# An FNO block and a dilation on one core: the first layer's product with x and its spectral rows as one pass of 32x32 matmuls

## The chip, the cores and the metric

The kernel runs on 1 core of one Trainium2 chip. The metric is the device time of one execution in microseconds (us). Several runs of each kernel are timed, and the median is given. One more execution is profiled, and its trace is what the profile is read from.

## The reference, cut to what matters

The input x has 8 images of 8 channels and 256 x 256 pixels. There are two stages, each with a group norm in front and a residual behind it.

```
x = x + L0(gn(x))        # lift 2 -> 10 channels per group, 4 Fourier layers, two pointwise layers
x = x + dilate(gn(x))    # maximum of a 3x3 window, border -2

L0(x):
  h = W0 @ [x, gridx, gridy] + b0                    # 4 groups, each 2 channels and 2 grids -> 10
  for i in 0..3:
    h1 = irfft2(R_i * rfft2(h), 12 + 12 rows and 12 columns of modes kept)
    h  = h1 + (W_i @ h + b_i);  h = swish(h) if i < 3
  h = swish(W_fc1 @ h + b)                           # 10 -> 128 per group
  return W_fc2 @ h + b                               # 128 -> 2 per group
```

The lift is linear, so the kernel never stores its result: layer 0 takes x itself, with the product of the two weights (`wc`), and the grids and biases enter as two extra rows of the spectral part.

## The kernel before, in words

The state of one image is the tile `h`: 128 partitions, 11 chunks (`NCH`), 4 quarters and 512 pixels, that is two rows of the image. A strip of 32 partitions holds 3 blocks of 10 channels. All data are float32, and each matmul of the program shows as two LDWEIGHTS and two MATMUL instructions in the profile.

Each image passes through four layers (`layers`, L505). Before a layer, `spectrum_h` (or, for layer 0, `spectrum_x`, L218) and `mix` (L345) compute the modes of the layer's output and write them to `fz`. There column 24 of the 32 columns holds a constant and column 25 a ramp. `rows_of` (L390) expands them to one set of 32 coefficients for each image row, in `zt`; it uses all 32 columns of `fz` against the table `rowg`. The columns 26 to 31 are zero.

`layer` (L416) then goes over the 11 chunks. `burst(c)` (L442) makes the layer's output for a chunk in two PSUM tiles. In layer 0 it first multiplies x by `wcn` (L449: 16 matmuls with 6 rows, 32 columns of weights and 512 pixels), where `wcn` is `wc` times the norm's factor (L476). Then it adds the spectral part (L455: 8 matmuls of the coefficients `zt`, 32 rows by 128, with the waves `binv`, 256 columns, 32 rows of which 26 are not zero). In the layers 1 to 3 the first product is with the state itself (L452). ACT applies the activation and writes `h` back in place (L461; L463 in layer 3). `turn(c-1)` (L424) transposes the chunk before, and `transform(c-2)` (L437) takes its row transform for the next layer.

After layer 3 a chunk goes to HBM (`stored`, L465). The two pointwise layers, `head` (L568), read it back in 256 KB tiles `hs` (L580) and work in 128 steps an image, two matmul groups (L588, L610) and two activations (L590) a step; a DVE addition (L615) follows every second step. These steps are woven into the layers of the next image: a generator yields numbers, and the main loop (L698 to L731) runs so many steps of `head` in between (`CHUNK` = 2, 1, 1 per chunk in the first three layers, `LAST` = 2 in layer 3). The dilation (`dilate`, L639) follows in the layers after that. It works in pieces of two rows: one transfer in (`yin`, L646), eight or so DVE operations, one transfer out (L674), both on POOL's queue. The start of the next image's layer 0, `spectrum_x` and its `mix`, runs within layer 3 of the image before (`start`, L498).

PE, DVE and ACT take their instructions in the order in which the program writes them (`manual_schedule`). The framework orders the DMA queues of SP and POOL itself, by its own estimate of when each transfer can begin. `read_x` (L467) loads the rows of x into `h`, 4 transfers of 6 rows by 8 KB for each chunk, all on SP's queue. They are written at the head of layer 0, and a chunk of `h` is free for them once the image before has stored it. SP's queue also has the stores, the `hs` loads, the spectral weights `t` (L342), x for the norm (L73) and x for the residual (L603).

One pool of four PSUM tiles (`ps_z`, two banks each) serves everything: a burst, a turn and a head step's L588 take two each, all else takes one.

Of the kernel before, what the change touches and what calls it, by code (L numbers as in the profile page):

```python
# [20 lines left out]
G = 4  # L21
# [17 lines left out]
STEPS = 128  # L39
CHUNK = (2, 1, 1)  # L40
LAST = (2,)
SIDE = 4.2


@with_exitstack
def fno_dilate_kernel(ctx: ExitStack, tc: tile.TileContext, a: dict, out: bass.AP):
# [42 lines left out]
    fc0c = load("fc0c", (128, 3))  # L89
    wbd = load("wbd", (128, WID, G))  # L90
    wt = load("wt", (128, 4, G, 32))
    eh0 = load("eh0", (128, 3, 2, 32), nc.sync)
    xe = load("xe", (128, 6, G, 5), nc.sync)
    wext = const.tile([128, G, WID, 5], F32, tag="c_wext", name="c_wext")
# [10 lines left out]
    edge = load("edge", (128, 4))  # L105

    h = const.tile([128, NCH, NQ, PIX], F32, tag="h", name="h")
    yin = const.tile([128, DR + 2, HW + 2], F32, tag="yin", name="yin")
    nc.vector.memset(yin, -BIG)
    y_rows = [dram.tile([C * HW + 2, HW], F32, tag=f"y{i}", bufs=1, name=f"y_rows{i}") for i in range(2)]  # L110
# [7 lines left out]

    def softplus(t, n, name):
        e = const.tile([128, n], F32, tag=f"{name}_e", name=f"{name}_e")
# [5 lines left out]
        sp = const.tile([128, n], F32, tag=f"{name}_sp", name=f"{name}_sp")  # L128
# [3 lines left out]
        rs = const.tile([128, n], F32, tag=f"{name}_rs", name=f"{name}_rs")  # L132
# [6 lines left out]
    sp_p, rs_p = softplus(beta_p, 4, "bp")  # L139
    sp_a, rs_a = softplus(beta_a, 4 * G, "ba")  # L140
    io = const.tile([128, 4 * G], F32, tag="io", name="io")
    nc.vector.tensor_copy(io[:, 0:4], sp_a[:, 0:4])
    nc.vector.tensor_tensor(io[:, 4:12], sp_a[:, 4:12], rs_a[:, 0:8], ALU.mult)
# [3 lines left out]
        nc.vector.tensor_scalar(w2[:, g, :], w2[:, g, :], rs_a[:, 12 + g : 13 + g], None, ALU.mult)  # L147


    wc = const.tile([128, 32], F32, tag="wc", name="wc")  # L150
    p = ps_z("p_wc")
    for g in range(G):
        mm(p[32 * g : 32 * g + 6, 0, :32], fc0x[part(g), :], wt[part(g), 0, g, :], start=True, stop=True)
# [10 lines left out]
    cv = const.tile([3, WID, G], F32, tag="cv", name="cv")  # L164
# [180 lines left out]
    def mix(b, l, out_):  # L345

        s = [sb.tile([128, 3, G, 2, WID], F32, tag=f"S{i}", bufs=1, name=f"S{i}_{b}_{l}") for i in range(2)]
        bt, sw = out_["bt"], out_["sw"]
        for k in range(3):
            for k2 in range(2):  # L350
                pr = turned[:, 2, 1024 * k2 : 1024 * k2 + 800].rearrange("p (g m i) -> p g m i", g=G, i=WID)
                nc.vector.tensor_tensor(  # L352
                    pr, sw[k], bt[:, k2, k].unsqueeze(2).to_broadcast([128, G, 2 * WID, WID]), ALU.mult)
                yield 0.7
                nc.vector.tensor_reduce(  # L355
                    s[k2][:, k].rearrange("p g s o -> p (g s o)"),
                    pr.rearrange("p g m i -> p (g m) i"), AX.X, ALU.add,
                )
                if k == 0 and k2 == 1:
                    sw.append(load_sw(l, 2))  # L360
                yield 0.7
        f = sb.tile([128, 2, 3, G, WID], F32, tag="F", bufs=1, name=f"F_{b}_{l}")
        nc.vector.tensor_tensor(f[:, 0], s[0][:, :, :, 0, :], s[1][:, :, :, 1, :], ALU.subtract)
        nc.vector.tensor_tensor(f[:, 1], s[0][:, :, :, 1, :], s[1][:, :, :, 0, :], ALU.add)
        yield 0.5

        p = ps_a(f"p_f_{b}_{l}")
        for slot in range(2):
            for n, (table, part_of) in enumerate(((0, slot), (1 + slot, 1 - slot))):
                for q in range(4):  # L370
                    mm(p[part(q), 120 * slot : 120 * slot + 120], fold[part(q), table, :],
                       f[part(q), part_of].rearrange("p k g o -> p (k g o)"), start=n == 0, stop=n == 1)
        nc.vector.tensor_copy(fz[0:32, :, :, 24], cz[:, l])
        if l == 0:
            mr = out_["mr"]
            d = sb.tile([128, 1], F32, tag="d", name=f"dm_{b}")
            nc.vector.tensor_tensor(d, mr[:, 0:1], mr[:, 1:2], ALU.mult)
            mm(p[0:1, 240 : 240 + WID * G], d, wm.rearrange("p o g -> p (o g)"), start=True, stop=True)
            nc.vector.tensor_tensor(
                fz[0:1, :, :, 24], fz[0:1, :, :, 24],  # L380
                p[0:1, 240 : 240 + WID * G].rearrange("p (o g) -> p o g", o=WID), ALU.add)
        if l < 2:
            nc.vector.tensor_copy(fz[0:32, :, :, 25], cz[:, 4 if l == 0 else 3])
        for q in range(4):
            dst = fz[part(q), :, :, 6 * q : 6 * q + 6].rearrange("p o g k -> p k g o")
            src = p[part(q), :240].rearrange("p (k g o) -> p k g o", g=G, o=WID)
            copy(q, dst, src)
        yield 2.5
# [24 lines left out]
            yield 0.7  # L413


    def layer(b, l, out_, stored, side):  # L416
        group_in_f = l % 2 == 1

# [22 lines left out]

        def burst(c):  # L442
            pair = [ps_z(f"p_z_{b}_{l}_{c}_{i}") for i in range(2)]
            for f in range(NQ):
                for q in range(NQ):
                    o = pair[q // 2][part(f), q % 2, :]
                    if l == 0:
                        k = slice(32 * q, 32 * q + 6)
                        mm(o, wcn[k, :], h[k, c, f, :], start=True, stop=False)  # L449
                    else:  # L450
                        g = f if group_in_f else q
                        mm(o, wt[part(q), l, g, :], h[part(q), c, f, :], start=True, stop=False)  # L452
            for s in range(2):
                for q in range(NQ):
                    mm(pair[q // 2][:, q % 2, HW * s : HW * (s + 1)],  # L455
                       zt[part(q), 2 * c + s].rearrange("p f o -> p (f o)"), binv[part(q), :],
                       start=False, stop=s == 1)
            for i in range(2):
                dst = h[:, c, 2 * i : 2 * i + 2, :]
                if l < 3:  # L460
                    nc.scalar.activation(dst, pair[i], AF.Silu)  # L461
                else:
                    nc.scalar.activation(dst, pair[i], AF.Identity, bias=bias3)  # L463
            if l == 3:
                nc.sync.dma_start(stored[c], h[:, c].rearrange("p f w -> p (f w)"))  # L465

        def read_x(c):  # L467
            for g in range(G):
                nc.sync.dma_start(
                    h[32 * g : 32 * g + 6, c].rearrange("p f w -> p (f w)"), a["xp"][b, c, g])  # L470
# [48 lines left out]
    spare = h.rearrange("p c f w -> p (c f w)")  # L519
# [228 lines left out]
def _tables():  # L748
# [40 lines left out]
    binv[:, at + 3] = -c * np.sin(_angle(np.outer(ky, w)))  # L789
    binv[:, 2 * NM] = 1.0  # L790
    binv[:, 2 * NM + 1] = line


    planes = [np.broadcast_to(line[:, None], (HW, HW)), np.broadcast_to(line, (HW, HW)), np.ones((HW, HW))]
    xe = np.zeros((4, 32, 2, 3, G, 5))
    for j, v in enumerate(planes):
# [83 lines left out]
```

## Time and profile before

| what | us |
|---|---|
| median of 3 runs (4305.38 to 4307.73) | 4307.59 |
| the profiled execution | 4309.43 |
| its span, first to last instruction | 4307.7 |
| L590 ACT, 2048 activations, mean 1.025 | 1968.9 |
| L588 PE, matmuls of the first pointwise layer | 1191.6 |
| L610 PE, matmuls of the second | 986.7 |
| L424 PE, transposes | 525.8 |
| L455 PE, spectral part, all four layers, 5632 instructions | 408.6 |
| L452 PE, product with the state, layers 1 to 3 | 317.0 |
| L449 PE, product with x, layer 0, 2816 instructions | 115.0 |

HBM carries 344.65 MB in all, a mean of 80 GB/s; the mean granted clock of TensorE is 0.982 of full speed. Busy time is the union of a group's instructions. Matmuls overlap each other, so a group's mean length times its count says little, and its place in time is better read from the timeline, where equal instructions in a row are merged: start, length, engine, line, what it writes and reads, how many. The brackets give idle time of that engine before it and what ended it. In the table by stage a row has the stretch and its length, the busy time of PE, of its weight loads, of DVE, ACT and POOL, then the granted clock, the share of the DMA engines and GB/s.

### The profile page before, as it was taken

What the parts mean: (1) busy time and instruction counts of PE and PEld (TensorE: products, weight loads), DVE (VectorE), ACT (ScalarE), POOL (GpSimd) and SP (SyncE); (2) the same over time, 40 slices, a digit from 0 to 9 for tenths busy, and PEclk for the clock granted to TensorE, in tenths of its full rate; (3) what the DMA queues carried; (4) which work ended last, traced back from release to release, by engine and by line L of the source; (5) the groups of instructions that cost most, each with busy time, mean ns of one, the idle gap of its engine ahead of it and who ended that gap; (6) DMA issues with size and microseconds to landing.
All of it is one profiled execution on the core that took longest, in us unless ns stands there. A gap on an engine that the chain in (4) does not pass through costs nothing. (4 is left out here: it accounts for less than half of the span.)

```text
span 4307.7 us, 115455 instructions
## 1 busy us (share of the span) xinstructions
PE 4089.1 (95%) x52330; PEld 1925.6 (45%) x52330; DVE 2297.3 (53%) x3424; ACT 2772.9 (64%) x2886; POOL 117.0 (3%) x202
## 2 busy tenths in 40 slices
PE   5877999999999999999999999999999999999997
PEld 3544454444443444434444354444454444444222
DVE  4444544555655555655556555655655555654433
ACT  3435656766667666576666756667666766567887
POOL 1000000000000000000000000000000000000000
PEclk8988999999999999999999999999999999999999
DMA  2014101332114221242112511134111332114321
GB/s 78 13 40 151 53 28 43 135 103 62 55 53 161 87 62 52 75 171 58 52 59 81 182 42 53 50 104 159 55 45 53 136 120 62 48 57 147 109 60 46
DMA packets 113682, 344.65 MB, mean 80 GB/s; under 512 B 15611, under 2 KB 18107, under 8 KB 97768
## 3 DMA queue, kind: packets, MB, share of 16 engines
q1 hardware_dynamic: 95000, 276.18, 20.3%
q0 software_dynamic: 18192, 61.08, 4.3%
q8 instruction: 411, 6.73, 0.7%
q14 instruction: 79, 0.65, 0.1%
HBM read 213.21 MB, written 123.74 MB: 78 GB/s over the span
## 5 line engine op out<-in xcount | busy, mean ns | idle before, releaser
L590 ACT ACTIVATE act<-p_fc 128x1024 f32<-128x1024 f32 x2048 | 1968.9, 1025 | 1202.4 <-PE p_fc L588 1200.6
L588 PE MATMUL p_fc<-hs,c_w 32*128 32x512 f32 x8192 | 1191.6, 633 | 15.3 <-DVE turned L194 8.6
L610 PE MATMUL p_fc<-act,c_w 128*32 128x512 f32 x8192 | 986.7, 597 | 38.9 <-ACT act L590 25.6
L194 DVE COPY turned<-p_t 128x1024 f32<-128x1024 f32 x495 | 584.6, 1219 | 707.7 <-PE p_t L424 707.0
L588 PEld LDWEIGHTS p_fc<-hs,c_w 32*128 32x128 f32 x8192 | 383.6, 183 | 622.8 <-issue 240.9
L461 ACT ACTIVATE h<-p_z 128x1024 f32<-128x1024 f32 x528 | 512.9, 1023 | 117.4 <-PE p_z L455 116.7
L424 PE MATMUL p_t<-ident,h 128*128 128x128 f32 x4224 | 525.8, 278 | 0.0
L615 DVE TENSOR_TENSOR y<-p_fc,y 128x512 f32<-128x512 f32 x392 | 270.7, 690 | 474.9 <-PE p_fc L610 473.0
L610 PEld LDWEIGHTS p_fc<-act,c_w 128*32 128x32 f32 x8192 | 229.9, 109 | 647.4 <-issue 333.0
L424 PEld LDWEIGHTS p_t<-ident,h 128*128 128x128 f32 x4224 | 463.3, 142 | 98.5 <-ACT act L590 64.7
L455 PE MATMUL p_z<-c_binv,zt 32*128 32x256 f32 x5632 | 408.6, 404 | 1.0 <-ACT zt L192 1.0
L455 PEld LDWEIGHTS p_z<-c_binv,zt 32*128 32x128 f32 x5632 | 258.3, 185 | 304.4 <-issue 292.7
L452 PE MATMUL p_z<-h,c_wt 32*32 32x512 f32 x8448 | 317.0, 601 | 0.0
L437 PE MATMUL p_d<-turned,c_fw 128*32 128x240 f32 x4224 | 268.1, 371 | 4.1 <-ACT act L590 2.1
L194 DVE COPY zt<-p_g 128x264 f32<-128x264 f32 x300 | 159.0, 626 | 139.8 <-PE p_g L397 75.0
L463 ACT ACTIVATE h<-p_z,c_bias 128x1024 f32<-128x1024 f32 x176 | 186.6, 1111 | 26.4 <-PE p_z L455 25.9
L355 DVE TENSOR_REDUCE S<-turned 128x80 f32<-128x800 f32 x192 | 188.8, 983 | 5.0
L352 DVE TENSOR_TENSOR turned<-t,B 128x800 f32<-128x800 f32 x192 | 188.4, 981 | 0.5 <-DMA t<-in_spw 0.4
L452 PEld LDWEIGHTS p_z<-h,c_wt 32*32 32x32 f32 x8448 | 72.3, 103 | 190.1 <-ACT act L590 85.7
L437 PEld LDWEIGHTS p_d<-turned,c_fw 128*32 128x32 f32 x4224 | 109.6, 108 | 100.4 <-issue 39.1
L194 DVE COPY turned<-p_at 88x1024 f32<-88x1024 f32 x90 | 101.7, 1155 | 73.8 <-PE p_at L313 73.8
L438 DVE COPY zt<-p_d 128x240 f32<-128x240 f32 x264 | 105.5, 400 | 51.1 <-PE p_d L437 51.1
(170 smaller groups left out, 2023.8 us busy)
## 6 DMA issues: line engine op xcount, KB each, us to landing
stored<-h SPq DMA_DIRECT2D x88, 1024.0 KB
hs<-stored SPq DMA_DIRECT2D x352, 256.0 KB
t<-in_spw SPq DMA_DIRECT2D x96, 400.0 KB
yin<-y_rows POOLq DMA_DIRECT2D x56, 512.0 KB, 4.7
h<-in_xp SPq DMA_DIRECT2D x352, 48.0 KB
turned<-in_x SPq DMA_DIRECT2D x16, 1024.0 KB
y<-in_x SPq DMA_DIRECT2D x56, 256.0 KB
y_rows<-y POOLq DMA_DIRECT2D x56, 256.0 KB, 2.4
```

The lines of the kernel that those rows point to most:

```text
L194: nc.vector.tensor_copy(dst, src)
L352: nc.vector.tensor_tensor(pr, sw[k], bt[:, k2, k].unsqueeze(2).to_broadcast([128, G, 2 * WID, WID]), ALU.mult)
L355: nc.vector.tensor_reduce(s[k2][:, k].rearrange("p g s o -> p (g s o)"), pr.rearrange("p g m i -> p (g m) i"), AX.X, ALU.add,)
L424: nc.tensor.transpose(t[:, i // 4, 128 * (i % 4) : 128 * (i % 4 + 1)], h[:, c, i // 2, 256 * (i % 2) + 128 * v : 256 * (i % 2) + 128 * (v ...
L437: mm(p[part(g), :240], fw[:, v, :], m[:, :, :, : NBLK * WID], start=v == 0, stop=v == 1)
L452: mm(o, wt[part(q), l, g, :], h[part(q), c, f, :], start=True, stop=False)
L455: mm(pair[q // 2][:, q % 2, HW * s : HW * (s + 1)], zt[part(q), 2 * c + s].rearrange("p f o -> p (f o)"), binv[part(q), :], start=False, s ...
L461: nc.scalar.activation(dst, pair[i], AF.Silu)
L588: mm(pair[g // 2][:, g % 2, :], w1[part(g), blk, :], hs[k][part(g), :], start=True, stop=True)
L590: nc.scalar.activation(act[:, 2 * i : 2 * i + 2, :], pair[i], AF.Silu)
L610: mm(acc[part(g), :], w2[:, g, 15 - rb - i : 47 - rb - i], act[:, g, :], start=i == 0, stop=i == 1)
L615: nc.vector.tensor_tensor(y, sums, y, ALU.add)
```

## The change

In layer 0 the two products become one. The 32 rows of a strip of `h` now hold 26 rows of waves (the first 26 rows of `binv`, repeated for the 8 image rows of a chunk) and 6 rows of x. The weight of x becomes six more columns of `fz`, 26 to 31, which `rows_of` spreads to `zt` through three new rows of `rowg`. A burst is 2 x 16 matmuls of 32 x 32 weights from `zt` with 256 columns of `h`, each its own accumulation group; L455 no longer runs in layer 0.

The waves come from a new table in HBM by 4 transfers of 26 x 8 KB for each chunk, on POOL's queue. The x rows stay on SP's queue, 4 transfers a chunk, now to the partitions 26 to 31 of each strip. Both are written in the program for the first four chunks ahead of `rows_of`, and for the chunk c+4 ahead of burst c.

The new columns of `fz` are made once an image in the `mix` of layer 0: a DVE scaling (`wsel`), 4 small matmuls into two PSUM tiles and two DVE copies. `wcn` goes. At the start of the program there are three more DVE operations (`ws`, `wk`) and one more table; a few small start-up tiles move into a part of `h`.

```diff
+    xrow = load("xrow", (128, 38))
...
-    wc = const.tile([128, 32], F32, tag="wc", name="wc")
+    wc = spare[:, 22400:22432]
...
+    ws = spare[:, 22472:22482]
+    nc.vector.tensor_tensor(ws, wc[:, 0:WID], wc[:, WID : 2 * WID], ALU.add)
+    nc.vector.tensor_tensor(ws, ws, wc[:, 2 * WID : 3 * WID], ALU.add)
+    wk = const.tile([128, WID, 6], F32, tag="wk", name="wk")
+    nc.vector.tensor_tensor(
+        wk, ws.unsqueeze(2).to_broadcast([128, WID, 6]),
+        xrow[:, 0:6].unsqueeze(1).to_broadcast([128, WID, 6]), ALU.mult)
...
             nc.vector.tensor_tensor(
                 fz[0:1, :, :, 24], fz[0:1, :, :, 24],
                 p[0:1, 240 : 240 + WID * G].rearrange("p (o g) -> p o g", o=WID), ALU.add)
+
+            wsel = sb.tile([128, 32], F32, tag="wsel", bufs=1, name=f"wsel_{b}")
+            nc.vector.tensor_scalar(wsel, xrow[:, 6:38], mr[:, 1:2], None, ALU.mult)
+            pair = [ps_z(f"p_wk_{b}_{i}") for i in range(2)]
+            for g in range(G):
+                mm(pair[g // 2][0:32, g % 2, : 6 * WID], wsel[part(g), :],
+                   wk[part(g)].rearrange("p o i -> p (o i)"), start=True, stop=True)
+            for i in range(2):
+                nc.vector.tensor_copy(
+                    fz[0:32, :, 2 * i : 2 * i + 2, 26:32].rearrange("p o g i -> p g o i"),
+                    pair[i][0:32, :, : 6 * WID].rearrange("p g (o i) -> p g o i", o=WID))
...
+    def read_x(b, c):
+
+        for g in range(G):
+            nc.gpsimd.dma_start(
+                h[32 * g : 32 * g + 26, c].rearrange("p f w -> p (f w)"), a["wave"])
+            nc.sync.dma_start(
+                h[32 * g + 26 : 32 * g + 32, c].rearrange("p f w -> p (f w)"), a["xp"][b, c, g])
...
-            for f in range(NQ):
-                for q in range(NQ):
-                    o = pair[q // 2][part(f), q % 2, :]
-                    if l == 0:
-                        k = slice(32 * q, 32 * q + 6)
-                        mm(o, wcn[k, :], h[k, c, f, :], start=True, stop=False)
...
+            if l == 0:
+
+                for s in range(2):
+                    cols = slice(HW * s, HW * (s + 1))
+                    for f in range(NQ):
+                        for q in range(NQ):
+                            mm(pair[q // 2][part(f), q % 2, cols], zt[part(q), 2 * c + s, f, :],
+                               h[part(q), c, f, cols], start=True, stop=True)
...
-        if l == 0:
-            for c in range(NCH):
-                read_x(c)
-            wcn = sb.tile([128, 32], F32, tag="wcn", bufs=1, name=f"wcn_{b}")
-            nc.vector.tensor_scalar(wcn, wc, out_["mr"][:, 1:2], None, ALU.mult)
         room = 0.0
         yield ()
         for c in range(NCH):
+            if l == 0 and c + AHEAD < NCH:
+                read_x(b, c + AHEAD)
             burst(c)
...
+            if l == 0:
+                for c in range(AHEAD):
+                    read_x(b, c)
             yield from rows_of(b, l)
             yield from layer(b, l, d, stored, then if l == 3 else iter(()))
...
+    for blk in range(NBLK):
+        rowg[0, 26 + blk, blk] = real[blk]
...
+        "xrow": xrow.reshape(128, 38), "wave": np.tile(binv[0, :26], (1, 2 * NQ)),
```

More of the change, by code (lines that the diff above doesn't have):

```diff
@@ L41 @@
 LAST = (2,)
+AHEAD = 4
 SIDE = 4.2
@@ L107, in fno_dilate_kernel @@
     h = const.tile([128, NCH, NQ, PIX], F32, tag="h", name="h")
+    spare = h.rearrange("p c f w -> p (c f w)")
     yin = const.tile([128, DR + 2, HW + 2], F32, tag="yin", name="yin")
@@ L117, in fno_dilate_kernel, with softplus @@
     nc.vector.memset(fz, 0.0)
-    def softplus(t, n, name):
-        e = const.tile([128, n], F32, tag=f"{name}_e", name=f"{name}_e")
+    def softplus(t, n, at):
+        e = spare[:, at + 0 * n : at + 1 * n]
         nc.vector.tensor_scalar(e, t, -1.0, None, ALU.mult)
@@ L127, in softplus @@
         nc.scalar.activation(e, e, AF.Ln)
-        sp = const.tile([128, n], F32, tag=f"{name}_sp", name=f"{name}_sp")
+        sp = spare[:, at + 1 * n : at + 2 * n]
         nc.vector.tensor_scalar(sp, t, 0.0, None, ALU.max)
@@ L131, in softplus @@
         nc.vector.tensor_scalar(sp, sp, 1e-20, None, ALU.max)
-        rs = const.tile([128, n], F32, tag=f"{name}_rs", name=f"{name}_rs")
+        rs = spare[:, at + 2 * n : at + 3 * n]
         nc.vector.tensor_scalar(rs, sp, 1.1, None, ALU.mult)
@@ L135, in softplus @@
         return sp, rs
-    sp_p, rs_p = softplus(beta_p, 4, "bp")
-    sp_a, rs_a = softplus(beta_a, 4 * G, "ba")
+    sp_p, rs_p = softplus(beta_p, 4, 22300)
+    sp_a, rs_a = softplus(beta_a, 4 * G, 22320)
     io = const.tile([128, 4 * G], F32, tag="io", name="io")
@@ L163, in fno_dilate_kernel @@
         nc.vector.tensor_scalar(wm[32 * g : 32 * g + 2, :, g], wc[32 * g : 32 * g + 2, :WID], -1.0, None, ALU.mult)
-    cv = const.tile([3, WID, G], F32, tag="cv", name="cv")
+    cv = spare[:3, 22432:22472].rearrange("p (o g) -> p o g", o=WID)
+    ws = spare[:, 22472:22482]
[5 more added lines that the diff above has]
+        xrow[:, 0:6].unsqueeze(1).to_broadcast([128, WID, 6]), ALU.mult)
     nc.vector.tensor_tensor(
@@ L443, in burst @@
             pair = [ps_z(f"p_z_{b}_{l}_{c}_{i}") for i in range(2)]
-            for f in range(NQ):
-                for q in range(NQ):
-                    o = pair[q // 2][part(f), q % 2, :]
-                    if l == 0:
-                        k = slice(32 * q, 32 * q + 6)
[L449 to L457, printed above, removed]
+            if l == 0:
[5 more added lines that the diff above has]
+                               h[part(q), c, f, cols], start=True, stop=True)
+            else:
+                for f in range(NQ):
+                    for q in range(NQ):
+                        mm(pair[q // 2][part(f), q % 2, :], wt[part(q), l, f if group_in_f else q, :],
+                           h[part(q), c, f, :], start=True, stop=False)
+                for s in range(2):
+                    for q in range(NQ):
+                        mm(pair[q // 2][:, q % 2, HW * s : HW * (s + 1)],
+                           zt[part(q), 2 * c + s].rearrange("p f o -> p (f o)"), binv[part(q), :],
+                           start=False, stop=s == 1)
             for i in range(2):
@@ L465, in burst @@
                 nc.sync.dma_start(stored[c], h[:, c].rearrange("p f w -> p (f w)"))
[L467 to L470, printed above, removed]
-        if l == 0:
-            for c in range(NCH):
-                read_x(c)
-            wcn = sb.tile([128, 32], F32, tag="wcn", bufs=1, name=f"wcn_{b}")
-            nc.vector.tensor_scalar(wcn, wc, out_["mr"][:, 1:2], None, ALU.mult)
         room = 0.0
@@ L516, in layers @@
         yield from then
-    spare = h.rearrange("p c f w -> p (c f w)")
     ya = spare[:, : 18 * (HW + 2)].rearrange("p (r w) -> p r w", r=18)
@@ L791, in _tables @@
     binv[:, 2 * NM + 1] = line
+    xrow = np.zeros((4, 32, 38))
+    for i in range(6):
+        xrow[:, i, i] = 1.0
+        xrow[:, i, 6 + 26 + i // 2] = 1.0
     planes = [np.broadcast_to(line[:, None], (HW, HW)), np.broadcast_to(line, (HW, HW)), np.ones((HW, HW))]
```

## The prediction

> **What bounds the kernel now.** I read the page first, then one stretch of the middle layers in the timeline, then the table by stage.
>
> ```profile
> PE 4089.1 (95%) x52330; PEld 1925.6 (45%) x52330; DVE 2297.3 (53%) x3424; ACT 2772.9 (64%) x2886; POOL 117.0 (3%) x202
> ```
>
> TensorE is busy for 95% of the span, and every other engine has a third or more to spare. A busy PE is not proof, so here is one chunk of layer 0, image 3 (start, length, engine, line):
>
> ```profile
> 1480.61 0.27 PEld L449 LDWEIGHTS p_z<-h,wcn 6*32 6x32 f32 x32 [0.76 <-DVE y L615]
> 1480.61 1.18 PE L449 MATMUL p_z<-h,wcn 6*32 6x512 f32 x32
> 1480.77 1.94 ACT L590 ACTIVATE act<-p_fc 128x1024 f32<-128x1024 f32 x2 [3.75 <-PE p_fc L588]
> ...
> 1481.72 1.15 PE L455 MATMUL p_z<-c_binv,zt 32*128 32x256 f32 x16
> ...
> 1482.80 1.97 PE L424 MATMUL p_t<-ident,h 128*128 128x128 f32 x16
> 1482.90 1.94 ACT L461 ACTIVATE h<-p_z 128x1024 f32<-128x1024 f32 x2 [0.19 <-PE p_z L455]
> ...
> 1484.69 1.02 PE L437 MATMUL p_d<-turned,c_fw 128*32 128x240 f32 x16
> ```
>
> Each PE group starts before the one ahead of it has ended, and none has an idle time in brackets: PE's own order sets the pace here. What a group costs is therefore the distance from its start to the next group's start: 1.11 us for L449, 1.08 for L455, 1.89 for L424, 0.95 for L437 (the next L588 starts at 1485.64).
>
> **Part 1: the spectral pass leaves layer 0.** Now a burst is L449 (16 matmuls of 512 columns, each 2 instructions) and then L455 (8 of 256). Afterwards it is 32 matmuls of 32x32 by 256 columns: 64 instructions. Per 32x32 tile of the array that is 4 rounds of 256 columns, where L449 has 2 rounds of 512: the same 1024 columns. L455 is four rounds of 256 columns too (16 instructions on four row strips), and takes 1.08. So I take 1.11 us, the row of the same tiles and columns. From below: L424 moves 16x128 = 2048 columns in 1.89, so 1024 take 0.94. From above: were the price one of instructions, 1.11/32 = 35 ns each, 64 would cost 2.22. Against that stands the group of smallest matmuls:
>
> ```profile
> 872.59 0.75 PE L279 MATMUL p_xs<-turned,c_eh 128*32 128x24 f32 x64 [0.88 <-DVE turned L272]
> 873.27 1.14 PE L588 MATMUL p_fc<-hs,c_w 32*128 32x512 f32 x8
> ```
>
> 64 instructions with their weight loads in 0.68 us: issuing is no limit at 1.11. The saving is L455's place, 1.08 us, in 11 chunks of 8 images: 88 x 1.08 = **-95 us** (bounds: 0.94 makes it -110; 2.22 makes it +3).
>
> Weight loads double from 16 to 32 pairs of the small kind. The PEld row above issues all 32 within 0.27 us, while the first round's matmuls (588 ns median on L449) still run on all four row strips, so loads hide behind running matmuls. The Trainium skill ("TensorE: Matmul & The Clock Gate", Part 3, The mechanism) says that a weight load overlaps running matmuls only when its row group differs; by that rule the three later rounds would each show a load of about 0.10 us, an estimated 88 x 0.3 = 26 us less gain. The row differs from the rule, and I go by the row.
>
> **Part 2: what is late next.** All four PSUM tiles are in use after a burst: two from L588, two from the burst. L424 takes the two that ACT empties at 1481.79 and 1482.71. PE will want them at 1481.72 and some 0.95 later, L437 wants the first burst tile at 1483.7 when ACT frees it at 1483.7, and the next step the second at 1484.65, when ACT ends it. PE and ACT are then level, and hand-overs show: I take 0.15 us a chunk, **+13 us**. From below 0, by the present row in which PE never waits; from above 0.5, about half an activation (0.97), +44 us.
>
> **Part 3: four small products per image in the first mix** (a DVE scaling, 8 PE instructions, two DVE copies). The place:
>
> ```profile
> 897.66 0.23 PE L378 MATMUL p_f<-c_wbd,dm 128*1 128x40 f32 x2
> 897.82 0.33 PEld L588 LDWEIGHTS p_fc<-hs,c_w 32*128 32x128 f32 x8
> ...
> 897.93 0.21 DVE L379 TENSOR_TENSOR fz<-fz,p_f 1x40 f32<-1x40 f32 x1 [1.02 <-PE p_f L378]
> 898.07 0.19 DVE L383 COPY fz<-c_cz 32x40 f32<-32x40 f32 x1
> 898.16 2.41 DVE L194 COPY fz<-p_f 32x240 f32<-32x240 f32 x4
> ```
>
> Today PE goes straight on to L588. The scaling stands on DVE behind L379, so PE waits with L588, L610 and all else behind it: from 897.82 to the scaling's end (898.07 + 0.22, as L476) and about 0.15 of hand-over, 0.6 us; then 8 instructions at L371's rate (32 in 0.95) 0.25. The DVE copies are half of one L194 copy each, some 0.35, and the four copies behind them end about 1.4 us later, which holds a PSUM tile that PE's next steps want. PE's wait for that is between 0 and the 2.4 us of those copies; I take 1.1, the middle. Together 2.0 us an image, **+16 us** (bounds 0.25 to 3.3 us, +2 to +26). The scaling L476 goes (0.21 us of DVE, hidden now, nothing). The first burst needs zt at once instead of 1.2 us later; its copies end at 915.34 and L449 starts at 915.51: nothing.
>
> At the start, three more DVE operations of 0.14 to 0.2 us lie on a DVE that is gapless from 16.9 to 20.7: **+0.5**; one more table load of 0.55 us on POOL ends long before its use. The small tiles moved into h cost nothing: same operations.
>
> **Part 4: the loads.** 352 new transfers of 26 x 8 KB on POOL's queue, 75 MB. By the page's DMA table the POOL queue's 61.08 MB took 4.3% of 16 engines, 2964 engine-us, so a chunk's 0.85 MB takes 41 engine-us: 2.6 us of all 16. POOL issues such a transfer in 0.54 (L674), 2.2 us a chunk. SP keeps its 352 loads of 48 KB. The stages (last columns: clock, DMA share, GB/s):
>
> ```profile
> 1433.50:1517.50 84.00, 83.03 (x1060) 41.90 (x1060) 40.58 (x55) 53.05 (x55) 1.29 (x2) 0.98 0.11 31
> ...
> 816.00:900.00 84.00, 79.02 (x1018) 31.36 (x1016) 43.67 (x72) 68.78 (x71) 0.54 (x1) 1.00 0.56 194
> ```
>
> The first is layer 0, the second layer 3 of the image before, where SP now issues the x loads (from 822.20 to 903 us, while layer 0 runs from 915.5), each as soon as its chunk is stored. If the new loads run in layer 0, the share goes from 0.11 to about 0.11 + 11 x 2.6/84 = 0.45: ample. In layer 3 it becomes 0.90, and the cover is distance: chunk 0 is loaded 80 us ahead of its burst. POOL's other work has slack: a yin transfer issued at 1489.27 lands in 4.7 us and is read at 1503.23. I cost the loads at **0**; SP issues as many as before, so no gain is hidden here, and the upper end is the second rival's +146. The Trainium skill ("DMA: Bandwidth & Descriptors", Issuing engines are not separate DMA queues) says that two issuing engines add no bandwidth, only issue time; no row here has two queues full, so that stays a warning.
>
> **Sum.** The profiled execution took 4309.4 us (span 4307.7 and 1.7 around it): 4309.4 - 95 + 13 + 16 + 0.5 = 4243.9. The median of the runs lies 1.8 below that execution, so I forecast **4242 us**.
>
> **Rivals.**
> - *ACT takes PE's place* (hand-over at 0.5 a chunk, mix at its upper bound): 4242 + 31 + 10 = 4283. For it: four activations in a row, level with PE. Against: ACT is busy 53 of 84 us in that stage.
> - *Slower: SP's chain in layer 3.* SP stores a chunk, waits until it has landed, issues its x loads, and only then stores the next:
>
> ```profile
> 824.41 0.35 SPq L465 DMA_DIRECT2D stored<-h  x1
> 830.83 0.96 SPq L469 DMA_DIRECT2D h<-in_xp  x3
> 831.89 0.35 SPq L465 DMA_DIRECT2D stored<-h  x1
> ```
>
> Stores follow each other in 7.8 us ((896.28 - 818.01)/10), and by the list of waits SP's stores waited 177.9 us for ACT in all, 2.0 us for each of 88. If the new loads run there and lengthen the chain by more than that, the states and spectral weights queued behind come late, and DVE and PE stop. Lengthened by 2.6 (all of the transfer time) the excess is 0.6 x 77 chunks = 46 us: 4288. Shared badly, at 1.5 times that (3.9), 1.9 x 77 = 146: **4388**. It is slower than before from 2.9 us a chunk on. For it: share 0.90. Against: the weights issued at 880.27 are read at 889.89, and the loads would mostly pass before the next store's data.
> - *Not what it says: instructions, not columns, have the price* (2.22 us a burst): 4309.4 + 3 + 13 + 16 + 0.5 - 1.8 = 4340. L279 speaks against it.
> - *Better:* 0.94 a burst, no hand-over, mix 0.25: 4309.4 - 110 + 2 + 0.5 - 1.8 = 4200.
>
> **How the numbers follow.** About 0.2% (9 us) is what can be told from no change. Chances: forecast, within 4225 to 4262, 0.60; better 0.08; ACT, or SP's chain just past its slack (4262 to 4299), 0.16; within 0.2% 0.04; instructions 0.03; SP's chain beyond 2.9 us 0.09. Faster 0.84, same 0.04, slower 0.12. The range, 4208 to 4297, leaves out part of the better case and the last three.
>
> **What would show it.** Right: in layer 0 the burst's distance to L424 is near 1.1 us, with no second group, and PE idle is small and ends on ACT; one gap of about 0.6 us on PE at the first mix; POOL and SP waits end nothing on PE. Wrong: a burst of 1.5 us or more; PE or DVE waiting for the new loads, for hs or t; stores more than 8.5 us apart in layer 3.

## The result and the profile after

The changed kernel takes **4398.91 us** (median of 6 runs, 4396.17 to 4402.15) where the kernel before takes 4306.49 in the same comparison: a ratio of 1.0217, 95% interval 1.0204 to 1.023. It is slower by 92 us. The prediction was 4242 us, faster. The profiled execution has a span of 4400.4 us.

Line numbers have moved: the burst of layer 0 is L480, the products of layers 1 to 3 are L485 and L489 (before L452 and L455), the turn is L454 (L424), the transform L467 (L437), the head's groups are L616 and L638 (L588, L610) with ACT's L618 (L590), the wave loads are L441, the x loads L443 (L469), the stores L499 (L465), `hs` L608 (L580), the spectral weights `t` are loaded in L353 (L342) and multiplied in L363 (L352).

The page after, engines: TensorE does less work (42 us) in a longer span.

```profile
PE 4046.8 (92%) x53802; PEld 1921.8 (44%) x53802; DVE 2303.7 (52%) x3443; ACT 2766.0 (63%) x2886; POOL 295.5 (7%) x555
```

To find where the time went, I cut the span at the bursts' activations: a layer lasts from its first to its last one, a boundary from the last one of layer 3 to the first one of the next image's layer 0 (each counted by its start; images are counted from 0). Summed over the images (seven boundaries), from the two profiled executions, in us:

| | start | layer 0 | boundaries 3 to 0 | all else | span |
|---|---|---|---|---|---|
| before | 72.7 | 601.7 | 171.9 | 3461.4 | 4307.7 |
| after | 82.0 | 537.2 | 313.2 | 3468.0 | 4400.4 |
| difference | +9.3 | -64.5 | **+141.3** | +6.6 | +92.7 |

So layer 0 does get shorter, and twice that is lost where layer 3 hands over to the next image. Here is one chunk of layer 0 in the timeline after, the answer to the chunk shown in the prediction:

```profile
1517.94 1.01 PEld L480 LDWEIGHTS p_z<-h,zt 32*32 32x32 f32 x64 [0.76 <-ACT act L618]
1517.95 1.49 PE L480 MATMUL p_z<-h,zt 32*32 32x256 f32 x64
...
1518.11 1.94 ACT L618 ACTIVATE act<-p_fc 128x1024 f32<-128x1024 f32 x2 [0.99 <-PE p_fc L616]
1519.37 1.73 PEld L454 LDWEIGHTS p_t<-ident,h 128*128 128x128 f32 x16 [0.41 <-ACT act L618]
1519.37 1.97 PE L454 MATMUL p_t<-ident,h 128*128 128x128 f32 x16
...
1521.27 1.02 PE L467 MATMUL p_d<-turned,c_fw 128*32 128x240 f32 x16
```

The second group is gone, and PE has no idle time in brackets (PE's rows are TensorE's matmuls, PEld's its weight loads). But from L480 to L454 it is 1.42 us, not the 1.11 that L449 had: the loads (PEld) now run for 1.01 us instead of 0.27.

The table by stage, for image 2's layer 3, its boundary and image 3's layer 0 (in each row the stretch, its length, busy PE, PEld, DVE, ACT, POOL, then clock, DMA share, GB/s), and below it layer 3 and the boundary before, of image 1:

```profile
1366.00:1443.70 77.70, 73.48 (x944) 29.54 (x938) 42.24 (x67) 63.15 (x65) 13.44 (x27) 1.00 0.69 201
1443.70:1490.90 47.20, 26.62 (x248) 11.45 (x250) 16.26 (x33) 16.40 (x18) 8.81 (x19) 0.75 0.70 206
1490.90:1562.20 71.30, 70.52 (x1154) 37.29 (x1153) 39.06 (x53) 49.33 (x54) 3.45 (x6) 1.00 0.30 79
```

```profile
816.00:893.50 77.50, 72.71 (x940) 28.95 (x934) 40.10 (x61) 62.93 (x64) 0.54 (x1) 1.00 0.56 192
893.50:917.90 24.40, 24.01 (x227) 10.21 (x230) 12.48 (x28) 16.56 (x19) 1.31 (x2) 1.00 0.60 181
```

Layer 3 itself is as long as before. The boundary is 47.2 us instead of 24.4, with PE busy for 26.6 of it at a granted clock of 0.75. The DMA share is 0.7, not 1. The timeline of that boundary shows what PE waits for:

```profile
1445.07 0.35 SPq L499 DMA_DIRECT2D stored<-h  x1
...
1455.07 0.27 SPq L443 DMA_DIRECT2D h<-in_xp  x1
1455.39 0.35 SPq L353 DMA_DIRECT2D t<-in_spw  x1
...
1456.55 0.35 SPq L499 DMA_DIRECT2D stored<-h  x1
...
1461.79 0.99 DVE L363 TENSOR_TENSOR turned<-t,B 128x800 f32<-128x800 f32 x1 [21.61 <-DMA t<-in_spw]
...
1466.65 1.82 PE L382 MATMUL p_f<-F,c_fold 32*32 32x120 f32 x32 [19.72 <-DVE F L374]
...
1469.60 2.50 PE L616 MATMUL p_fc<-hs,c_w 32*128 32x512 f32 x8
```

Read it from the bottom. PE stood 19.72 us for DVE, DVE stood 21.61 us for the spectral weights `t`, and SP issued those weights at 1455.39, only once the x load in front of them could go, at 1455.07, which is when the store of 1445.07 had landed. The first group of L616 behind the pause takes 2.50 us instead of 1.14; the clock is down (granted 0.50 in the stretch from 1450.5 to 1473).

The lists of waits over the whole run, where the columns are total us, times, longest. The first two are after, of the engines and of SP's queue; the last two are before.

```profile
POOL h L441 <- DMA stored<-h: 617.1, 38, 274.5
PE p_f L382 <- DVE F L374: 157.2, 10, 21.3
DVE turned L363 <- DMA t<-in_spw: 130.9, 8, 21.6
```

```profile
SPq L443 <- DMA stored<-h: 588.7, 73, 11.0
...
SPq L499 <- ACT h L497: 114.9, 29, 18.2
```

```profile
SPq L469 <- DMA stored<-h: 292.8, 67, 6.2
SPq L465 <- ACT h L463: 177.9, 53, 18.9
```

```profile
DVE turned L352 <- DMA t<-in_spw: 0.4, 1, 0.4
```

DVE's wait for `t` was 0.4 us in all before. SP's x loads wait twice as long for their stores, and the longest wait grew from 6.2 to 11.0 us: a store now takes longer to land. In image 2's layer 3 the stores are issued at 1368.21 to 1478.82, that is 11.1 us apart (110.61/10) where they were 7.8 apart before.

### The profile page after: what moved, and what is told of

It is laid out like the page before. It is cut to its first block, busy times and chain, and to the rows that moved or that the text cites. A ratio compares the mean times of both kernels' runs of the same rounds, so it can differ in the third digit from the quotient of the medians.

```text
span 4400.4 us, 119480 instructions
## 1 busy us (share of the span) xinstructions
PE 4046.8 (92%) x53802; PEld 1921.8 (44%) x53802; DVE 2303.7 (52%) x3443; ACT 2766.0 (63%) x2886; POOL 295.5 (7%) x555
## 5 line engine op out<-in xcount | busy, mean ns | idle before, releaser
L618 ACT ACTIVATE act<-p_fc 128x1024 f32<-128x1024 f32 x2048 | 1969.3, 1025 | 1300.5 <-PE p_fc L616 1298.6
L616 PE MATMUL p_fc<-hs,c_w 32*128 32x512 f32 x8192 | 1205.6, 637 | 20.6 <-DVE turned L205 8.5
L638 PE MATMUL p_fc<-act,c_w 128*32 128x512 f32 x8192 | 993.1, 601 | 36.8 <-ACT act L618 25.9
L616 PEld LDWEIGHTS p_fc<-hs,c_w 32*128 32x128 f32 x8192 | 389.5, 184 | 634.0 <-issue 237.7
L454 PE MATMUL p_t<-ident,h 128*128 128x128 f32 x4224 | 519.3, 276 | 0.1
L638 PEld LDWEIGHTS p_fc<-act,c_w 128*32 128x32 f32 x8192 | 231.4, 110 | 653.3 <-issue 345.8
L454 PEld LDWEIGHTS p_t<-ident,h 128*128 128x128 f32 x4224 | 457.0, 141 | 103.4 <-ACT act L618 70.6
L485 PE MATMUL p_z<-h,c_wt 32*32 32x512 f32 x8448 | 318.3, 602 | 0.7 <-issue 0.7
L489 PE MATMUL p_z<-c_binv,zt 32*128 32x256 f32 x4224 | 304.6, 401 | 0.6 <-ACT zt L203 0.6
L489 PEld LDWEIGHTS p_z<-c_binv,zt 32*128 32x128 f32 x4224 | 193.4, 184 | 228.2 <-issue 220.8
L467 PE MATMUL p_d<-turned,c_fw 128*32 128x240 f32 x4224 | 268.1, 371 | 4.8 <-DVE turned L205 2.7
L363 DVE TENSOR_TENSOR turned<-t,B 128x800 f32<-128x800 f32 x192 | 188.6, 982 | 131.0 <-DMA t<-in_spw 130.9
L441 POOL DMA_DIRECT2D h<-in_wave x352 | 177.3, 507 | 1052.9 <-DMA stored<-h 617.1
L382 PE MATMUL p_f<-F,c_fold 32*32 32x120 f32 x1024 | 41.5, 311 | 182.5 <-DVE F L374 157.2
L485 PEld LDWEIGHTS p_z<-h,c_wt 32*32 32x32 f32 x8448 | 72.3, 103 | 192.2 <-ACT act L618 87.2
L467 PEld LDWEIGHTS p_d<-turned,c_fw 128*32 128x32 f32 x4224 | 109.7, 108 | 101.1 <-issue 38.9
```

What stands on the lines that cost most here:

```text
L363: nc.vector.tensor_tensor(pr, sw[k], bt[:, k2, k].unsqueeze(2).to_broadcast([128, G, 2 * WID, WID]), ALU.mult)
L454: nc.tensor.transpose(t[:, i // 4, 128 * (i % 4) : 128 * (i % 4 + 1)], h[:, c, i // 2, 256 * (i % 2) + 128 * v : 256 * (i % 2) + 128 * (v ...
L467: mm(p[part(g), :240], fw[:, v, :], m[:, :, :, : NBLK * WID], start=v == 0, stop=v == 1)
L485: mm(pair[q // 2][part(f), q % 2, :], wt[part(q), l, f if group_in_f else q, :], h[part(q), c, f, :], start=True, stop=False)
L489: mm(pair[q // 2][:, q % 2, HW * s : HW * (s + 1)], zt[part(q), 2 * c + s].rearrange("p f o -> p (f o)"), binv[part(q), :], start=False, s ...
L616: mm(pair[g // 2][:, g % 2, :], w1[part(g), blk, :], hs[k][part(g), :], start=True, stop=True)
```

## The experiments

**Theory A:** the loss is one of order on SP's queue. The new wave loads make a store land some 4 us later; each x load on SP waits for its store; everything behind it, the spectral weights above all, waits too. **Rival B:** the waves simply take too much of the transfer engines, wherever the loads stand. **Rival C:** the change to four chunks ahead, not the waves, has put the loads in the wrong place.

Each time is a median beside that of the kernel before on the same chip (4305.7 to 4308.8); stages are from the profiled execution of each, as above.

| run | us | ratio, 95% interval | start | layer 0 | boundaries | all else |
|---|---|---|---|---|---|---|
| e1_pool_in_order | 4331.85 | 1.0052 (1.0037 to 1.0067) | 81.6 | 553.3 | 227.8 | 3469.0 |
| e2_x_on_pool | 4274.34 | 0.9923 (0.9907 to 0.994) | 75.9 | 539.2 | 190.6 | 3464.9 |
| e3_before_waves | 4431.10 | 1.0283 (1.0268 to 1.0299) | 78.9 | 595.1 | 281.8 | 3468.1 |
| e4_ahead_11 | 4467.86 | 1.0367 (1.0351 to 1.0382) | 82.1 | 599.2 | 320.1 | 3464.7 |
| f1_one_weight | 4255.63 | 0.9880 (0.9865 to 0.9894) | 75.0 | 524.7 | 195.5 | 3459.4 |
| f2_narrow | 4381.78 | 1.0176 (1.0159 to 1.0193) | 74.9 | 638.8 | 195.6 | 3467.5 |
| f3_row_group_runs | 4281.12 | 0.9939 (0.9924 to 0.9953) | 76.3 | 546.0 | 196.1 | 3460.2 |
| f4_stores_on_pool | 4273.04 | 0.9919 (0.9904 to 0.9933) | 75.8 | 546.6 | 173.8 | 3469.2 |
| g1_stores_on_act | 4283.14 | 0.9951 (0.9938 to 0.9965) | 76.2 | 539.3 | 183.4 | 3483.1 |
| g2_act_stores_x_on_sp | 4458.17 | 1.0354 (1.0339 to 1.0368) | 81.0 | 538.5 | 230.0 | 3611.3 |

### POOL's loads in the written order

```diff
-    with tc.manual_schedule(engines={PE, DVE, ACT}):
+    with tc.manual_schedule(engines={PE, DVE, ACT, POOL}):
```

> The changed kernel with POOL's queue also kept in the program's order, so that the wave loads of chunk 4 on start at layer 0 and not behind each store of layer 3; nothing else differs. Theory A (the wave transfers, running in layer 3, slow the stores; SP's queue waits for each store ahead of its x loads, and the third tile of spectral weights t stands behind them; DVE and PE stop for it about 20 us in each of 7 images): the stop shrinks to under 3 us an image, time about 4260 to 4280. Theory B (the merged burst or the added products in the mix cost more than they save): time stays within 4385 to 4400, since neither is touched.

4331.85 us, between the two numbers. With the waves of chunk 4 on taken out of layer 3, the boundaries fall from some 44 to 30.5 us (image 0's is 44.8), and DVE's wait for `t` from 130.9 to 48.2 us. Layer 0 is 16 us longer than after. So part of the loss is where the waves run, and about 6 us a boundary is left while the x loads stay on SP. The sixteen waves of the first four chunks still run in layer 3: in image 2's they go out from 1402 to 1418, and the x load behind the store of 1406.06 goes only at 1421.78.

### The x loads on POOL's queue

```diff
-            nc.sync.dma_start(
+            nc.gpsimd.dma_start(
                 h[32 * g + 26 : 32 * g + 32, c].rearrange("p f w -> p (f w)"), a["xp"][b, c, g])
```

> The changed kernel with the x rows on POOL's queue too, so that SP's queue no longer waits for a store ahead of t; as many bytes move in layer 3 as before. Theory A in the form that the order on SP's queue is at fault: t is issued when its buffer is free, DVE's wait for t under 20 us in all (130.9 in the changed kernel), time about 4250 to 4280. Theory A in the form that the DMA engines are simply full (t and the stores land late whatever the queue): 4370 to 4400, with DVE still waiting over 100 us for t.

4274.34 us: **faster than the kernel before by 0.77%**, with the waves still in layer 3. DVE's wait for `t`, and how long a store takes to land (the last number, median us, of the page's DMA issues):

```profile
DVE turned L363 <- DMA t<-in_spw: 19.0, 2, 16.4
```

```profile
stored<-h SPq DMA_DIRECT2D x88, 1024.0 KB, 9.7
```

The stores land as late as after, 9.7 us, and in layer 3 (1366 to 1450 us of this run) the share of the transfer engines is 0.78 with 233 GB/s, more than in the changed kernel. Yet SP goes on in the meantime:

```profile
1390.19 0.32 SPq L499 DMA_DIRECT2D stored<-h  x1
1397.51 0.33 SPq L353 DMA_DIRECT2D t<-in_spw  x1
1399.86 0.32 SPq L499 DMA_DIRECT2D stored<-h  x1
1400.27 0.38 SPq L608 DMA_DIRECT2D hs<-stored  x1
1405.31 0.33 SPq L353 DMA_DIRECT2D t<-in_spw  x1
1406.26 0.32 SPq L499 DMA_DIRECT2D stored<-h  x1
```

Six of the seven boundaries are 25.0 us, against 24.3 before. That is theory A, and B falls: more traffic, and no delay in those six (the seventh, image 0's, comes below). No run moves the x loads of the kernel before; with 0.4 us of waiting for `t`, little was to be gained there. The Trainium skill ("DMA: Bandwidth & Descriptors", Anatomy of one DMA — SWDGE (gpsimd) path) says that transfer engines never wait on semaphores; the waiting is done by the issuing sequencer before it dispatches. SP's queue here is a case of it: a load that waits keeps the ready one behind it from being issued.

### The waves in the kernel before

```diff
             nc.sync.dma_start(
...
+                nc.gpsimd.dma_start(
+                    h[32 * g + 6 : 32 * g + 32, c].rearrange("p f w -> p (f w)"), a["wave"])
```

> The kernel before with nothing but the wave loads added, on POOL's queue, into rows of h that layer 0 does not read; the output does not depend on them. Theory A: all of the loss comes from these transfers, so 4307 + 7 x 20 + 9 at the start, about 4440 to 4465. Theory B: the transfers are hidden, 4305 to 4315.

4431.10 us: 122 us more than the kernel before, a little under the 4440 to 4465 of theory A, and DVE's wait for `t` is 116.9 us instead of 0.4:

```profile
DVE turned L352 <- DMA t<-in_spw: 116.9, 8, 21.1
```

The old arithmetic, the old program place of the x loads, and the loss is there. Rival C falls; neither the new burst nor the four chunks ahead makes it.

### Eleven chunks ahead

```diff
-AHEAD = 4
+AHEAD = 11
```

> The changed kernel with AHEAD = 11: all loads written ahead of the first burst instead of four chunks ahead. Theory A with the framework's own ordering of the queues (each load goes out as soon as its chunk is stored, wherever it is written): no change, 4390 to 4410. If the distance of four chunks does hold loads back in the changed kernel: all of them now pile up in layer 3, 4410 to 4450.

Neither number was met: 4467.86 us, 69 more than after. The boundaries are about as after (320.1); layer 0 lost 62 us, and the list of PE's waits says to what:

```profile
PE p_fc L616 <- DMA hs<-stored: 78.1, 7, 26.0
```

The 26.0 us are in the boundary of image 0, where 29 x loads in a row stand on SP's queue ahead of the `hs` load. The six other waits, 52.1 us in all, lie in the layers 0 behind. In SP's queue behind image 2, for one, two stores and twelve x loads go out between the `hs` loads of 1479.42 and 1511.26; in the changed kernel one store and six x loads stand between those of 1457.00 and 1477.67. So the four chunks ahead do matter, in another way than I thought: they keep `hs` loads ahead of the late x loads. It is theory A with another victim.

### The burst: fewer pairs, more pairs, another order

Three kernels on top of e2 ask why a burst takes 1.425 us (the median of the distance from L480 to L454) and not 1.11.

```diff
-                for s in range(2):
...
+                for f in range(NQ):
+                    for q in range(NQ):
+                        mm(pair[q // 2][part(f), q % 2, :], zt[part(q), 2 * c, f, :],
+                           h[part(q), c, f, :], start=True, stop=True)
```

> The kernel with the x loads on POOL's queue (4274.3 us), with layer 0's burst as 16 matmuls of 512 columns, 32 load-and-multiply pairs where it has 64. Both image rows of a chunk get the first row's coefficients, so the second row's own are left out; columns, tiles, transfers and everything else stay. Theory: the burst's place of 1.425 us holds 0.31 us too much because of the number of its pairs (from about the 33rd on, pairs start 16.7 ns apart, behind a gap of 0.19 us). Then the burst falls to 1.11 us, as L449 of the kernel before, and the time falls by 88 x 0.31 = 27 us to about 4247. Rival: the price comes from the operands (32 rows of weights and data in each strip where L449 had 6). Then the burst stays near 1.42 us and the time near 4274.

4255.63 us; the burst has a median of 1.24 us. In the first image, which has no head steps beside it, it is 1.09. The timeline says where the 0.15 between them comes from:

```profile
1470.69 0.28 PEld L478 LDWEIGHTS p_z<-h,zt 32*32 32x32 f32 x32 [0.76 <-DVE y L641]
1470.69 1.18 PE L478 MATMUL p_z<-h,zt 32*32 32x512 f32 x32
1470.86 1.94 ACT L616 ACTIVATE act<-p_fc 128x1024 f32<-128x1024 f32 x2 [3.14 <-PE p_fc L614]
...
1471.93 1.77 PEld L454 LDWEIGHTS p_t<-ident,h 128*128 128x128 f32 x16 [0.96 <-ACT act L616]
```

The turn's first weight load waits for ACT: the first of the two activations ends about 1470.86 + 0.97 = 1471.83, and the turn starts 0.10 later. So 32 pairs take 1.09 us, as predicted from L449, and the hand-over then costs the 0.15 that was predicted too. With 64 pairs the burst outlasts ACT and the hand-over is hidden.

```diff
-                for s in range(2):
-                    cols = slice(HW * s, HW * (s + 1))
+                for s in range(4):
+                    cols = slice(HW // 2 * s, HW // 2 * (s + 1))
...
-                            mm(pair[q // 2][part(f), q % 2, cols], zt[part(q), 2 * c + s, f, :],
+                            mm(pair[q // 2][part(f), q % 2, cols], zt[part(q), 2 * c + s // 2, f, :],
```

> The kernel with the x loads on POOL's queue (4274.3 us), with each matmul of layer 0's burst cut in two of 128 columns: 128 pairs, the same columns in all, nothing left out. If pairs have a price of 16.7 ns once the first 32 or so are through, the burst goes to about 1.425 + 64 x 16.7 ns = 2.5 us, and the time to 4274 + 88 x 1.07 = about 4368. If columns have the price, it stays near 1.42 us and 4274. In between (a weight load that shows partly between rounds of half the length) the burst would lie between 1.42 and 2.5 us.

4381.78 us. An undisturbed burst takes 1.83 us:

```profile
1496.88 1.90 PE L480 MATMUL p_z<-h,zt 32*32 32x128 f32 x128
1498.71 1.97 PE L454 MATMUL p_t<-ident,h 128*128 128x128 f32 x16
...
1502.62 1.72 PE L480 MATMUL p_z<-h,zt 32*32 32x128 f32 x107
1506.23 0.47 PE L480 MATMUL p_z<-h,zt 32*32 32x128 f32 x21 [1.89 <-issue]
```

The same columns in 32, 64 and 128 pairs take 1.09, 1.425 and 1.83 us: a pair more costs 0.335/32 = 10 ns at first and 0.405/64 = 6 ns then. It is pairs that have a price, though less than the 16.7 ns that I had read from the second half of a burst. The Trainium skill ("TensorE: Matmul & The Clock Gate", Part 3, Measured speedup vs the span model) has about 4 ns of issue for each further tile, which by our estimate would make 0.13 and 0.26 us of the two steps; the runs show 0.335 and 0.405. The time rose by 107 us where 88 x 0.405 = 36 would follow: the rest is pauses like the last line's, in which PE waits for nothing that the profile shows. What they are stays open.

```diff
-                    for f in range(NQ):
-                        for q in range(NQ):
+                    for q in range(NQ):
+                        for f in range(NQ):
```

> The kernel with the x loads on POOL's queue (4274.3 us), with the two loops inside layer 0's burst exchanged: four matmuls in a row now share a row strip and differ in their column strip, where neighbours differed in their row strip; nothing is left out. If pairs in general have the price, whatever their place, nothing changes: 1.42 us and 4274. If a weight load can't run beside matmuls of its own row strip, most loads now show: 64 loads of 10 ns or more each, so the burst is longer by 0.3 us at the least, and the time 4300 or more.

4281.12 us, the burst 1.48 us instead of 1.425: 0.055 x 88 = 5 of the 7 us. The exchange puts 24 more of the 31 pairs of neighbouring matmuls of the program on a shared row strip, so such a neighbour costs 0.055/24, some 2 ns. The order of the strips is thus not what sets the 1.425 us. The rule that the prediction weighed (the Trainium skill, "TensorE: Matmul & The Clock Gate", Part 3, The mechanism: a weight load overlaps running matmuls only where its row group differs) is not settled by this run: in both orders each matmul's own two load-and-multiply pairs share a strip, and matmuls run on all four strips. Its estimate of 26 us less gain came close to 88 x 0.315 = 28; no run here shows that this is more than chance, and why a pair costs 6 to 10 ns stays open.

### The stores elsewhere

In e2 image 0's boundary is still 40.8 us, and 16.4 of DVE's 19.0 us of waiting are there. Without head steps that layer 3 lasts 41 us instead of 78, so its stores follow each other faster than they land.

```diff
-                nc.sync.dma_start(stored[c], h[:, c].rearrange("p f w -> p (f w)"))
+                nc.gpsimd.dma_start(stored[c], h[:, c].rearrange("p f w -> p (f w)"))
```

> The kernel with the x loads on POOL's queue (4274.3 us), with the stores of layer 3 on POOL's queue too, so that SP's queue no longer has any transfer that waits for layer 3's bursts. Theory (the spectral weights are late because they stand behind waiting transfers on SP's queue): the boundary behind image 0, the only one still late (40.8 us where the others have 25.0), falls to about 25, DVE's wait for the weights goes to about 0, and the time falls by 16 us to about 4258. Rival: the weights of image 0 are late because the stores and waves share the transfer engines with them; then the boundary stays near 40 and the time near 4274. The risk on the other side: a store that stands on POOL's queue behind a transfer of the dilation comes late, and the head's loads of the state with it; then PE waits for hs, and the time is above 4274.

4273.04 us, level with e2. The boundary fell to 24.0 us and DVE's wait for `t` to 2.1 us, as theory A has it; the waves now stand behind the stores on one queue, and a store lands in a median of 6.2 us instead of 9.7. Most of what it gained was given back: layer 0 is 7.4 us longer and the end 4.8 us. In layer 0 the loss lies in the first bursts (in image 4, one ends on 1.16 us of idle that the profile puts down to issue); whether the later loads cause it wasn't settled.

```diff
-                nc.sync.dma_start(stored[c], h[:, c].rearrange("p f w -> p (f w)"))
+                nc.scalar.dma_start(stored[c], h[:, c].rearrange("p f w -> p (f w)"))
```

> The kernel with the x loads on POOL's queue (4274.3 us), with the stores of layer 3 issued by ACT, each right behind the two activations that make its chunk, so that neither SP nor POOL has a store in its queue. Theory: the boundary behind image 0 (40.8 us) falls to about 25, as with the stores on POOL, and layer 0 stays at its 71.2 us an image, because the waves and x no longer stand behind stores that wait for ACT. ACT pays some 0.35 us a store, 3.9 us an image, in a stage where it is busy 60 of 84 us; if that is hidden the time is about 4274 - 16 = 4258. Rival: PE is released by ACT at each chunk of layer 3, so the issue shows in full: 88 x 0.35 = 31 us more, about 4289.

4283.14 us, between the two numbers: both happen. Image 0's boundary falls to 31.2 us, and layer 3 gets 21.7 us longer over the images (596.5 instead of 574.8). ACT spends 0.33 us on issuing each store, 88 x 0.33 = 29 us in all, so most of it shows.

The last one makes the same edit in the changed kernel, with the x loads left on SP.

> The changed kernel (4398.9 us), with only the stores of layer 3 moved from SP to ACT; the x loads stay on SP's queue, where each still waits until its chunk has been stored and its states loaded. If it is the waiting x loads that hold the spectral weights back, the weights stay late: the boundaries stay near 43 us and the time is 4380 to 4410. If the stores on SP were the matter, or the two together (store behind load, load behind store, one chain), the chain is cut: stores follow each other at ACT's pace, 7.8 us apart, the boundaries fall to 25 to 32 us and the time to 4260 to 4320.

Neither: 4458.17 us. The boundaries did fall to 28 to 35 us, but layer 3 takes 95 to 100 us in the images 1 to 6 instead of 78. By the profile the stores that ACT issues wait for x loads, and ACT's own work behind them:

```profile
1430.73 0.33 ACTq L499 DMA_DIRECT2D stored<-h  x1
1431.10 3.77 ACT L618 ACTIVATE act<-p_fc 128x1024 f32<-128x1024 f32 x4 [3.54 <-DMA h<-in_xp]
```

Over the run ACT's L618 waited 104.1 us in this way. Why a store should need an x load to have landed isn't settled. The run doesn't tell the stores and the x loads on SP apart, which it was made for; by the profile's releasers the wait has once more moved to what stands behind a waiting transfer.

## Why the prediction was wrong

The failed step is **Part 4**, "I cost the loads at **0**". What took its place is the prediction's own second rival, SP's chain in layer 3, to which it gave 9 in 100. The predicted change was -65.5 us (-95 + 13 + 16 + 0.5) and the measured one is +92.7, in the profiled executions. By the prediction's terms the 158 us between them are:

| step | predicted | measured | from |
|---|---|---|---|
| Part 1 and 2, layer 0 | -95 + 13 = -82 | -64.5 | stages |
| Part 3, mix | +16 | +5 | 7 x 0.7, e2's boundaries against before |
| start | +0.5 | +9.3 | stages |
| Part 4, loads | 0 | +136 | 141.3 of the boundaries less the mix |
| all else | 0 | +6.6 | stages |

**Part 4.** It named the loads' share of the engines (0.90 in layer 3; measured 0.69) and took the distance of 80 us to their own use for cover. The loads indeed hold up none of their own readers. What it missed is who else waits: the argument against the rival was that the new loads "would mostly pass before the next store's data". They don't. A wave load can only start when a store has landed, so it runs beside the next store, and that one lands late. The waves of one chunk are issued at the same time as the next store:

```profile
1385.97 2.00 POOL L441 DMA_DIRECT2D h<-in_wave  x4 [11.30 <-DMA stored<-h]
```

```profile
1386.53 0.35 SPq L499 DMA_DIRECT2D stored<-h  x1
```

The second argument, weights "issued at 880.27 are read at 889.89", counted one slot of slack as if the shift didn't add up from chunk to chunk.

The rival's size was off as well. At the measured 3.2 us a chunk (11.06 - 7.83) its formula gives (3.2 - 2.0) x 77 = 92 us, but the boundaries lost 136. The 2.0 us of slack was an average over all stores. After the change they still wait 114.9 us for ACT, 1.3 a store; only 0.7 of the 2.0 was ever used up. Of what is left, 18.2 + 7 x 6.8 = 65.8 us are waits of the first store of a layer 3, which do not help the later ones. Put back into the formula, the loss of 136/77 = 1.8 us a chunk would mean a slack of 1.4 us; that is an estimate, not a measurement.

**Part 1.** The mechanism was right and the term mis-sized: the burst is 1.425 us, not 1.11. From L449 and L455 to L480 a chunk falls from 2.19 to 1.425, 88 x 0.764 = -67 us instead of -95. The step that failed is the reading of L279, "issuing is no limit at 1.11", and of the PEld row: loads that lie within 0.27 us for 32 pairs take 1.01 us for 64. f1 has the columns and not the pairs, and there layer 0 takes 524.7 us, 77 less than before, where -82 was forecast.

**Part 2.** The hand-over of 0.15 us is real (f1), but shows only when the burst takes 1.09. The longer burst hides it, so the two terms are not to be added: 88 x (1.425 - 1.24) = 16 us is what the second 32 pairs cost beside the head steps, and f1 gained 14.5 in layer 0 (539.2 - 524.7).

**Part 3.** Here is its place in e2, to be held against L378 and L588 of before:

```profile
1415.65 0.23 PE L389 MATMUL p_f<-c_wbd,dm 128*1 128x40 f32 x2
...
1416.05 0.22 DVE L395 TENSOR_SCALAR wsel<-c_xrow,mr_x 128x32 f32<-128x32 f32 x1
...
1416.42 0.31 PE L398 MATMUL p_wk<-wk,wsel 32*32 32x60 f32 x8 [0.54 <-DVE wsel L395]
...
1416.75 1.45 PE L616 MATMUL p_fc<-hs,c_w 32*128 32x512 f32 x8
```

From L389 to L398 it is 0.77 us where L378 to L588 was 0.16, so PE's wait is 0.61 (predicted 0.6); the products take 0.33 (predicted 0.25). The third part, 1.1 us for PSUM tiles that DVE holds, does not exist: L616 starts with no wait. Of the 0.94 us some is made up later, and the boundary is longer by 0.7.

**The start** was costed by its DVE operations. The waves again have the larger part: with the waves alone (e3) the start is 6.2 us longer than before. Image 0's 44 go out from 19.45 us on, and DVE waits 7.69 us for a `t` tile that SP issued at 48.30.

## What to carry to other kernels

A transfer that waits for a semaphore (the signal that an engine or another transfer is done) holds back all that stands behind it on its queue. When a change adds traffic, first list what the queues carry in that stage, which entry waits, and what urgent load stands behind it; a free share of the transfer engines, 0.3 in layer 3 here, did not tell of it. Here one word, the queue of the x loads, turned 4398.9 into 4274.3 us.

Slack that is an average over waits can't be spent where the waits are not. And equal columns are not equal time: ask how many load-and-multiply pairs they come in.

## What was not expected of the hardware

- A pause of PE costs more than itself. After 19.72 us without work the granted clock is 0.75 over the boundary, and 0.50 from 1450.5 to 1473, and the first eight matmuls of L616 take 2.50 us instead of 1.14.
- 64 pairs of 32 x 32 weights and 256 columns take 1.425 us, 32 pairs of 512 columns 1.09, 128 pairs of 128 columns 1.83.
- 0.85 MB of waves to a chunk lengthen the landing of a 1 MB store from 6.4 us (824.41 to 830.83 before) to a median of 9.7 (e2), and the share of the transfer engines is then 0.7 to 0.8.
